# Quarter images for all groups: the second upsampling layer and the last layer of a preactivation chain of four convolutions

## The chip, the core and the metric

The kernel runs on one core of one Trainium2 chip. The metric is the device time of one execution in microseconds (us). A run's time is taken without a profiler; the profiled execution is a run of its own, with its own time.

## What is computed

The input is `x` of 16 samples, 32 channels, 128 x 128. Four layers follow each other, each with a normalisation before it and a residual around it: a recurrent layer along the diagonals (L0), an adder layer (L1: minus the sum of absolute differences between each 3 x 3 patch and each filter), a layer in the Hartley domain (L2: 32 x 32 modes are mixed), and a small encoder and decoder (L3). Only the end of L3 is touched by the change:

```python
def conv3x3(x, w, b):      # 3 x 3, padded, 32 -> 32 channels
def deconv2x2(x, w, b):    # 2 x 2 upsampling, 32 -> 32 channels
# five edge operators on x, normalised, 160 channels
y1 = maxpool2(conv1(edges))        # 64 x 64
y2, y3 = maxpool2(conv2(y1)), maxpool2(conv3(y2))   # 32 x 32, 16 x 16
y4 = conv4(y3)                     # 16 x 16
y5 = conv5(deconv1(y4))            # 32 x 32
y6 = conv6(deconv2(y5))            # 64 x 64
y7 = conv7(deconv3(y6))            # 128 x 128
# the output combines y7 with the normalised image
```

In the code a `deconv` and the `conv` behind it are one layer: `up5`, `up6` and `up7` compose their weights into 16 products of 32 x 32 channels (four output parities, four taps each) and small corrections at the image's edges.

## The kernel before

**Stages.** `stage0` does the recurrent layer (0 to about 690 us). `rest` does the others. In `Differences.run` each of the 16 images, in two halves, needs 72 tap arrays per half (2304 in all): relu(q - w) over 128 partitions and 8192 or 8320 elements, in float16. DVE makes some of them (`d_dve`, L760) and ACT the others (`d_act`, L757); PE sums each with 16 products (L647). DVE has three buffers for them, ACT two. Where PE would be idle between sums, products with zeros are put in (`keep_busy`, L677).

**Weaving.** The layers L2 and L3 work on groups of four samples (NG = 4). Their work is a generator, `After.work`, and the class `Weave` puts steps of it between the tap arrays. It keeps a planned time for PE, DVE and ACT. A step yields a positive number (PE time), a negative one (a wait) or `SUMMED` (wait until PE's sums are there), and adds its costs to `weave.dve` and `weave.act`; `later` and `on_act` put a step off. From the same plan comes the choice of the engine for each tap array. At the end `keep_order` fixes the order on every engine, so a wait at the head of an engine's queue holds all that stands behind it. Group g may start when image 4g + 3 is through; its parts in order are `forward` (loads `xh` at L1059 and products at L1110, mode mixing at L1221), `back` (L1295, L1345, residuals at L1320), `statistics` (L1491), `conv1` (L1874) with its pooled outputs, `small_layers` and `last`. Groups 0 to 2 are woven in; what is left of group 2 when the arrays end is played together with the whole of group 3 by `drain`, which takes the next step of whichever generator's planned time is lower. When group 2 is through, group 3 goes on alone (`weave.alone`).

**Layouts.** A tile with a plain layout has 4 samples x 32 channels on the partitions (`padded`). In a tile by quarters (`quartered`), the 128 partitions are 4 quarters of the image's rows x 32 channels, and the samples lie in the free dimension; `neighbours` copies each quarter's edge rows to the one next to it (L1812, L1814). Products are 32 x 32 blocks, 16 at a time: the row block of PE is a sample or a quarter, the column block is what becomes the output's partition block.

**up6.** Group 3 (`self.whole`) writes `y6` by quarters, through `to_quarters` and `evict` (L1789 on DVE, L1792 on ACT). Groups 0 to 2 write a plain `y6` through `upsampled` and `spread`: there the output's partition block is a parity (row, column), so that each bank of 512 sums is taken out in four pieces of 32 partitions, on DVE (L1778) or ACT (L1781). `up5` uses `spread` in all groups, with 256 elements a piece.

**The last layer.** Group 3 keeps its normalised image in SBUF, writes the output into it (`last_in_place`) and stores it by 8 rows of each quarter. Groups 0 to 2 read the normalised image back from DRAM by units of 32 rows (L1972, four transfers per unit, tiles `xr3`, two buffers): the partitions are four row blocks x 32 channels, the samples are in the free dimension. DVE combines (L2032), ACT adds the mean (L2002), and SP stores (L2011, sixteen transfers per unit). As the normalisation's numbers belong to a sample and channel, and the partitions do not have the samples here, a small product (L1984) with its operands (L1981, L1987) brings them into place first.

**SP's queue** carries nearly all transfers: the tiles `xq` and `q` of the adder layer, its stores, the group's loads and the output's stores, in one order. In the drain it carries the loads of group 3's image (L1282) ahead of group 2's `u_conv7` and `xr3`.

Of the kernel before, what the change touches and what calls it, by code (L numbers as in the profile page):

```python
# [7 lines left out]
F32 = mybir.dt.float32  # L8
F16 = mybir.dt.float16
I32 = mybir.dt.int32  # L10
AF = mybir.ActivationFunctionType
# [5 lines left out]
HW = H * W  # L17
# [945 lines left out]
class After:  # L963
# [16 lines left out]
    def work(self, groups):  # L980
        if 0 in groups:
            yield from self.prepare()
        for g in groups:
            with self.pool("g_sm") as sm:
                yield ("after", 4 * g + 3)
                if g not in self.scales:
                    yield -8.0
                self.stats3 = sm.tile([128, 2, 1], F32, name="stats3")
                self.shift3 = sm.tile([128, 1], F32, name="shift3")
                yield from self.forward(g)  # L990
                with ExitStack() as kept:
                    yield from self.encoder(g, kept)
                    if self.whole:
                        yield from self.last_in_place(g)
                    else:
                        yield from self.last(g, g + 1 if g + 1 in groups else None)

    def acc(self):

# [642 lines left out]
    def small_layers(self, cp, rp, y1, y2):  # L1642
# [3 lines left out]
        if not y1:  # L1646
            for n in ("conv3", "conv4"):
                wc[n] = replicated(nc, cp, self.a[n], 9, f"w_{n}")
            up5, up6 = self.up5.loaded(cp), self.up6.loaded(cp)
            y3 = self.quartered(cp, 16, "y3")  # L1650
            y4, y5 = (self.padded(cp, n, f"y{i}") for n, i in ((16, 4), (32, 5)))
            self.y6 = y6 = (self.quartered if self.whole else self.padded)(rp, 64, "y6")
            yield -7.0

        def conv(name, n, rows, pick, evict, taps=range(9), late=None):
# [93 lines left out]
            ),  # L1749
        )  # L1750
        yield from upsampled(y4, 16, up5, y5)
        yield from (to_quarters if self.whole else upsampled)(y5, 32, up6, y6)

    def padded(self, pool, n, name):
        nc, t = self.nc, pool.tile([128, n + 2, n + 2], F32, name=name)
# [15 lines left out]
    def spread(self, dst, src, blk, b, engine):  # L1771

        nc, weave = self.nc, self.weave
        for j in range(4):
            d, s = dst(slice(32 * blk, 32 * blk + 32), j), src[32 * j : 32 * j + 32]
            bj = b[32 * j : 32 * j + 32]
            if blk % 2 == 0 if weave.alone else engine is nc.vector:
                nc.vector.tensor_scalar(d, s, bj, None, ALU.add)  # L1778
                weave.dve += 0.3
            else:  # L1780
                nc.scalar.activation(d, s, AF.Identity, bias=bj)  # L1781
                weave.act += 0.45

    def evict(self, dst, src, b, blk, engine=None):

# [137 lines left out]
        for v in spreads:  # L1923
            weave.done(v)

    def last_in_place(self, g):

        nc, x = self.nc, self.image
        with self.pool("l_y") as yp:
            up = self.up7.loaded(yp)
            one = yp.tile([128, 1], F32, name="l_one")
            nc.vector.reciprocal(one, self.stats3[:, 1])
            nc.vector.tensor_scalar(one, one, up.bias, None, ALU.add)
            for unit in range(4):
                for pr in range(2):
                    acc = [self.acc() for _ in range(4)]
                    for pc in range(2):  # L1940
                        pick = lambda q: (2 * pr + pc, 16 * q + 4 * unit, 4, 256 * pc)
                        yield from up.round(self.y6, 64, acc, pick, 16)
                    yield SUMMED
                    for q in range(4):
                        first = 2 + 32 * q + 8 * unit + pr
                        v = x[:, first : first + 7 : 2, 2 : W + 2].rearrange("p r (w b) -> p r w b", b=2)
                        nc.vector.scalar_tensor_tensor(
                            v, acc[q].rearrange("p (b r w) -> p r w b", b=2, w=64), one, v, ALU.add, ALU.mult
                        )
                    yield -2.5  # L1950
                for q in range(4):
                    row = 32 * q + 8 * unit
                    v = x[:, 2 + row : 10 + row, 2 : W + 2]
                    nc.scalar.activation(v, v, AF.Identity, bias=self.stats3[:, 0])
                    to = self.out.offset + g * 4 * CHW + row * W
                    nc.sync.dma_start(bass.AP(self.out.tensor, to, [[HW, 128], [W, 8], [1, W]]), v)

    def last(self, g, following_group):

        nc, tc, cst, weave = self.nc, self.tc, self.cst, self.weave  # L1960
        with self.pool("l_y") as yp, self.pool("l_x", self.buffers["l_x"]) as xp:
            ahead = self.buffers["l_x"]
            y6 = self.y6
            up = self.up7.loaded(yp)

            def load(unit):
                xr = xp.tile([128, 4, 8 * PW], F32, name="xr3")
                t = self.d["xn"]
                for j in range(4):
                    first = t.offset + g * 128 * PADDED + (2 + 32 * unit + 8 * j) * PW  # L1970
                    rows = bass.AP(t.tensor, first, [[PADDED, 32], [32 * PADDED, 4], [1, 8 * PW]])
                    nc.sync.dma_start(xr[32 * j : 32 * j + 32], rows)  # L1972
                return xr

            def inner(x):
                return x.rearrange("p b (h w) -> p b h w", w=PW)[:, :, :, 2 : W + 2]

            xr = [load(unit) for unit in range(ahead)]

            rhs = yp.tile([128, 2, 4], F32, name="l_rhs")  # L1980
            nc.vector.tensor_tensor(rhs, bcast(self.stats3[:, :, 0], 2, 4), bcast(cst["m4_bc"], 1, 2), ALU.mult)  # L1981
            yield -2.0
            p = self.acc()
            nc.tensor.matmul(p[:, :8], cst["sel_c"], rhs.rearrange("p a b -> p (a b)"), start=True, stop=True)  # L1984
            yield SUMMED
            ms = yp.tile([128, 8], F32, name="l_ms")
            nc.vector.tensor_copy(ms, p[:, :8])  # L1987
            mean, istd = ms[:, 0:4], ms[:, 4:8]


            one = yp.tile([128, 4], F32, name="l_one")
            nc.vector.reciprocal(one, istd)
            nc.vector.tensor_scalar(one, one, up.bias, None, ALU.add)
            yield -4.0


            following = {}

            def done(x, unit):
                for blk in range(4):  # L2000
                    v = inner(x)[:, blk]
                    nc.scalar.activation(v, v, AF.Identity, bias=mean[:, blk : blk + 1])  # L2002
                weave.act += 4.4
                following[unit] = weave.later(4.0 if weave.alone else 14.0, lambda: store(x, unit))

            def store(x, unit):
                for blk in range(4):
                    for j in range(4):
                        first = self.out.offset + (g * 4 + blk) * CHW + (32 * unit + 8 * j) * W
                        rows = bass.AP(self.out.tensor, first, [[HW, 32], [W, 8], [1, W]])  # L2010
                        nc.sync.dma_start(rows, inner(x)[32 * j : 32 * j + 32, blk])  # L2011
                following[unit] = weave.later(10.0, lambda: reload(unit)) if unit + ahead < 4 else None

            def reload(unit):
                xr.append(load(unit + ahead))
                following[unit] = None

            def complete(unit):
# [2 lines left out]

            for unit in range(4):
                complete(unit - ahead)
                x = xr[unit]
                for pr in range(2):
                    acc = [self.acc() for _ in range(4)]
                    for pc in range(2):
                        yield from up.round(y6, 64, acc, lambda j: (2 * pr + pc, 16 * unit + 4 * j, 4, 256 * pc))
                    yield SUMMED
                    for blk in range(4):  # L2030
                        v = inner(x)[:, blk, pr::2].rearrange("p r (w b) -> p r w b", b=2)
                        nc.vector.scalar_tensor_tensor(  # L2032
                            v,
                            acc[blk].rearrange("p (b r w) -> p r w b", b=2, w=64),
                            one[:, blk : blk + 1],
                            v,
                            ALU.add,
                            ALU.mult,
                        )
                        weave.dve += 0.75  # L2040
                    yield -2.5
                following[unit] = weave.on_act(lambda x=x, unit=unit: done(x, unit))
# [168 lines left out]
```

## Time and profile before

| what | value |
|---|---|
| median of 3 runs | 6511.71 us (6506.15 to 6521.65) |
| the profiled execution's own time | 6506.94 us |
| its span, first to last instruction | 6505.2 us |
| busy: PE, DVE, ACT | 5343.1, 5475.0, 5312.8 us (82%, 84%, 82%) |
| tap arrays, on DVE and on ACT | 1673 and 631 |
| woven stage (arrays), about | 690 to 5651 us |
| group 2 and 3 together, group 3 alone | 5651 to 6042, 6042 to 6505 us |
| mean granted TensorE clock | 0.929 |

In the rows of the profile, a group of instructions has its line, engine and operation, then output <- input with partitions x elements, and the count after an x; behind the bar stand the busy time in us and the mean of one in ns, and behind the next bar the idle time of the engine just before such instructions, with what ended it. In a timeline the first number is the start and the second the length of a run of equal instructions, both in us. A matmul of 32-bit floats shows as two records, and so does its weight load. "issue" is a wait that no semaphore explains.

### The profile page before, as it was taken

To read this page: it belongs to the slowest core of one execution; us is meant where nothing else is said; L and a number is where in the kernel's file an instruction comes from. 1 tells how busy PE (TensorE), PEld (TensorE's weight loads), DVE (VectorE), ACT (ScalarE), POOL (GpSimd) and SP (SyncE) were. 2 spreads that over 40 slices of the span, in tenths; PEclk is the share of its full clock that TensorE was granted. 3 is DMA by queue.
4 is the path that set the end of the run, shared out by engine and by line. 5 is a ranking of instruction groups with operands and counts; after the bars stand their busy time and mean duration, and the time that the engine had idled before them with its cause. 6 is when DMAs were issued, how large, how long until landed. Compare 5 with 4: busy or idle time off the path is not lost.

```text
span 6505.2 us, 274662 instructions
## 1 busy us (share of the span) xinstructions
PE 5343.1 (82%) x129394; PEld 2805.1 (43%) x129394; DVE 5475.0 (84%) x6551; ACT 5312.8 (82%) x2816; POOL 65.6 (1%) x67
## 2 busy tenths in 40 slices
PE   3689677888877879998887889998878799977696
PEld 3576233344434433333344433334344443345594
DVE  7799899999999999999999889999989889744212
ACT  3899799999999989999999899999989899702001
POOL 0000000000000000000000000000000000000000
PEclk9999899999999889999989989999989899977898
DMA  7543323121154632222455522314545522344102
GB/s 314 218 173 126 91 51 82 46 57 45 32 140 124 197 120 87 66 74 68 110 166 165 176 79 70 97 42 92 146 128 172 171 58 62 101 139 121 35 4 65
DMA packets 366576, 700.87 MB, mean 108 GB/s; under 512 B 70852, under 2 KB 219332, under 8 KB 354564
## 3 DMA queue, kind: packets, MB, share of 16 engines
q1 hardware_dynamic: 357972, 648.87, 34.4%
q0 software_dynamic: 7040, 33.80, 1.6%
q8 instruction: 1012, 16.58, 1.1%
q14 instruction: 120, 0.98, 0.0%
q10 hardware_dynamic: 432, 0.64, 0.0%
HBM read 500.46 MB, written 182.69 MB: 105 GB/s over the span
## 4 chain that ended last, share of the span: by engine, by line
PE 41%; issue 25%; DVE 20%; ACT 8%; DMA 4%; SPq 1%; POOL 0%; DVEq 0%; ACTq 0%; POOLq 0%
PE acc L647 14%; PE acc L1874 13%; DVE d_dve L760 12%; ACT d_act L757 4%; PE acc L908 3%; PE pg L223 3%; ACT gt L237 2%; PE acc L1664 2%; ACT junk L198 1%; PE acc L1491 1%; PE acc L677 1%; DVE stat L124 1%; PE acc L662 1%; DMA v<-fold_d 1%; PE acc L1221 1%
## 5 line engine op out<-in xcount | busy, mean ns | idle before, releaser
L757 ACT ACTIVATE d_act<-q,neg 128x8192 f16<-128x8192 f16 (+1 forms) x631 | 4470.2, 7149 | 209.1 <-PE acc L647 190.1
L760 DVE TENSOR_SCALAR d_dve<-q,qw 128x8192 f16<-128x8192 f16 (+1 forms) x1673 | 3866.9, 2360 | 215.7 <-PE acc L647 195.1
L647 PE MATMUL acc<-d_dve,sel 128*32 128x512 f16 x26768 | 1862.5, 397 | 429.2 <-DVE d_dve L760 333.6
L647 PEld LDWEIGHTS <-sel 128*32 128x32 f16 x36864 | 984.7, 99 | 1968.1 <-issue 1291.7
L647 PE MATMUL acc<-d_act,sel 128*32 128x512 f16 x10096 | 713.7, 403 | 153.3 <-ACT d_act L757 142.4
L1874 PE MATMUL acc<-xp,wf 32*32 32x512 f32 x19200 | 721.1, 609 | 16.7 <-issue 15.8
L677 PE MATMUL acc<-q,zero 128*32 128x512 f16 x8584 | 582.7, 388 | 6.3 <-issue 6.3
L223 PE MATMUL pg<-h,wb 64*64 64x20 f32 (+15 forms) x8192 | 342.8, 306 | 61.0 <-DVE h L251 32.9
L237 ACT ACTIVATE gt<-pg,bias 128x20 f32<-128x20 f32 (+15 forms) x1024 | 332.6, 384 | 45.8 <-PE pg L223 43.5
L1874 PEld LDWEIGHTS acc<-xp,wf 32*32 32x32 f32 x19200 | 225.2, 103 | 315.9 <-issue 285.8
L908 PE MATMUL acc<-y,u_conv 32*32 32x256 f32 (+1 forms) x9984 | 313.0, 461 | 50.8 <-issue 33.8
L677 PEld LDWEIGHTS <-zero 128*32 128x32 f16 x8584 | 247.3, 99 | 229.3 <-issue 35.2
L1792 ACT ACTIVATE y<-pooled,b 128x128 f32<-128x128 f32 x112 | 39.7, 396 | 348.9 <-DVE pooled L1767 230.7
L223 PEld LDWEIGHTS pg<-h,wb 64*64 64x64 f32 x8192 | 252.8, 150 | 135.8 <-DVE h L251 79.5
L908 PEld LDWEIGHTS acc<-y,u_conv 32*32 32x32 f32 x9984 | 149.5, 111 | 151.3 <-issue 113.3
L223 PE MATMUL pg<-xn,wb 64*64 64x2 f32 (+63 forms) x4096 | 186.1, 292 | 27.9 <-issue 19.2
L1874 PE MATMUL acc<-image,wf 32*32 32x512 f32 x6400 | 207.3, 605 | 0.0
L1874 PEld LDWEIGHTS acc<-image,wf 32*32 32x32 f32 x6400 | 180.5, 103 | 24.1 <-issue 3.5
L1491 PE MATMUL acc<-xp 32*64 32x204 f32 (+2 forms) x6432 | 175.5, 341 | 13.5 <-issue 13.4
L1908 DVE TENSOR_TENSOR acc<-acc,cut 128x8 f32<-128x8 f32 x128 | 19.5, 166 | 194.0 <-PE acc L1874 194.0
L2002 ACT ACTIVATE xr<-xr,l_ms 128x1024 f32<-128x1024 f32 x48 | 51.5, 1145 | 152.3 <-DVE xr L2032 152.3
L1664 PE MATMUL acc<-y,w_conv 32*32 32x512 f32 (+2 forms) x4608 | 142.7, 476 | 26.5 <-issue 19.0
(248 smaller groups left out, 3891.8 us busy)
## 6 DMA issues: line engine op xcount, KB each, us to landing
q<-q_d SPq DMA_DIRECT2D x128, 536.2 KB, 9.7
xp<-xn_d SPq DMA_DIRECT2D x24, 2112.0 KB, 9.0
x_in<-in_x_dram SPq DMA_DIRECT2D x16, 2048.0 KB, 14.7
xn<-in_xs_dram SPq DMA_DIRECT2D x64, 512.0 KB, 7.2
res<-in_x_dram SPq DMA_DIRECT2D x64, 512.0 KB, 8.8
x_d<-res SPq DMA_DIRECT2D x64, 512.0 KB, 5.2
xq<-x_d SPq DMA_DIRECT2D x256, 128.0 KB, 4.4
xr<-x_d SPq DMA_DIRECT2D x256, 128.0 KB, 5.0
```

Of the source, the lines that this page charges most:

```text
L124: nc.vector.bn_stats(stat0[:, g, 8 * q + k, :], t[:, k * 512 : (k + 1) * 512])
L198: nc.scalar.activation(junk, flat(res, g)[:, 512 * half : 512 * half + 512], AF.Square, bias=away[:, g : g + 1], accum_out=squares[:, g, c ...
L223: nc.tensor.matmul(bank[c][q][64 * pair : 64 * pair + 64, :, :width], wb[half, 4 * kind + KIND[q]].rearrange("p b o -> p (b o)"), v[half], ...
L237: nc.scalar.activation(gt[:, q, :, :n], bank[c][q][:, :, :n], AF.Tanh if q == G else AF.Sigmoid, bias=bias[:, KIND[q] : KIND[q] + 1],)
L647: self.nc.tensor.matmul(acc[k][32 * j : 32 * j + 32, :], self.sel16[:, i // 9, :], d[:, row : row + 4, c : c + W], start=first, stop=last,)
L677: self.nc.tensor.matmul(acc[k][32 * j : 32 * j + 32, :], self.zero, q[:, :4, :W], start=False, stop=False)
L757: nc.scalar.activation(dst, src, AF.Relu, bias=self.neg[:, i : i + 1])
L760: nc.vector.tensor_scalar(dst, src, self.qw[:, i : i + 1], 0.0, ALU.subtract, ALU.max)
L908: nc.tensor.matmul(acc[blk][32 * j : 32 * j + 32, o : o + rows * n], t[part, 4 * par + tap, :], own[:, top : top + rows, left : left + n], ...
L1491: nc.tensor.matmul(gram[blk][j : j + width, at : at + n], xp[part, l, 2 + j : 2 + j + width], xp[part, rows, j : j + width + 4], start=sta ...
L1664: nc.tensor.matmul(acc[blk][32 * j : 32 * j + 32, : rows * n], wc[name][part, tap, :], pick(part, blk, j)[:, tap // 3 : tap // 3 + rows, t ...
L1874: nc.tensor.matmul(acc[blk][32 * j : 32 * j + 32, :], tap_of("all", tap)[rows], xp[rows, at + apart * j + kh : at + apart * j + kh + 4, kw ...
```

## The change

All groups now write `y6` by quarters: `to_quarters` with `evict` for everyone. `last_in_place` and `last` become one function. For groups 0 to 2 the last layer's partitions are now the samples and channels, a unit is 8 rows of each quarter, a load takes one transfer per unit (the same bytes) and a store four; the mean and the deviation are used as they are. In group 3 the addition of the mean and the stores are put off by `on_act`. `spread` tells the planner other costs.

```diff
@@ After.work
-                    if self.whole:
-                        yield from self.last_in_place(g)
-                    else:
-                        yield from self.last(g, g + 1 if g + 1 in groups else None)
+                    yield from self.last(g, g + 1 if g + 1 in groups else None)
@@ small_layers
-            self.y6 = y6 = (self.quartered if self.whole else self.padded)(rp, 64, "y6")
+            self.y6 = y6 = self.quartered(rp, 64, "y6")
...
-        yield from (to_quarters if self.whole else upsampled)(y5, 32, up6, y6)
+        yield from to_quarters(y5, 32, up6, y6)
@@ spread
-                weave.dve += 0.3
+                weave.dve += s.free_size() / 960 + 0.2
...
-                weave.act += 0.45
+                weave.act += s.free_size() / 960 + 0.25
@@ last
-    def last_in_place(self, g):
...
+    def last(self, g, following_group):
+        nc, weave = self.nc, self.weave
+        mean = self.stats3[:, 0]
+        with self.pool("l_y") as yp, ExitStack() as ring:
+            up, ahead = self.up7.loaded(yp), self.buffers["l_x"]
+            xr, following = [], {}
+            if not self.whole:
+                xp = ring.enter_context(self.pool("l_x", ahead))
+
+            def load(unit):
+                xr.append(xp.tile([128, 4, 8 * PW], F32, name="xr3"))
+                t = self.d["xn"]
+                first = t.offset + g * 128 * PADDED + (2 + 8 * unit) * PW
+                nc.sync.dma_start(xr[unit], bass.AP(t.tensor, first, [[PADDED, 128], [32 * PW, 4], [1, 8 * PW]]))
+
+            def rows(unit):
+                if self.whole:
+                    x = self.image[:, 2 : H + 2, :].rearrange("p (q r) w -> p q r w", q=4)
+                    return x[:, :, 8 * unit : 8 * unit + 8, 2 : W + 2]
+                return xr[unit].rearrange("p q (r w) -> p q r w", w=PW)[:, :, :, 2 : W + 2]
+
+            if not self.whole:
+                for unit in range(ahead):
+                    load(unit)
             one = yp.tile([128, 1], F32, name="l_one")
             nc.vector.reciprocal(one, self.stats3[:, 1])
             nc.vector.tensor_scalar(one, one, up.bias, None, ALU.add)
+            yield -4.0
+
+            def done(x, unit):
+                for q in range(4):
+                    nc.scalar.activation(x[:, q], x[:, q], AF.Identity, bias=mean)
+                    if self.whole:
+                        store(x, unit, q)
+                weave.act += 4.4
+                after = weave.later(4.0 if weave.alone else 14.0, lambda: stored(x, unit)) if not self.whole else None
+                following[unit] = after
+
+            def store(x, unit, q):
+                to = self.out.offset + g * 4 * CHW + (32 * q + 8 * unit) * W
+                nc.sync.dma_start(bass.AP(self.out.tensor, to, [[HW, 128], [W, 8], [1, W]]), x[:, q])
...
             for unit in range(4):
+                complete(unit - ahead)
+                x = rows(unit)
                 for pr in range(2):
                     acc = [self.acc() for _ in range(4)]
                     for pc in range(2):
                         pick = lambda q: (2 * pr + pc, 16 * q + 4 * unit, 4, 256 * pc)
                         yield from up.round(self.y6, 64, acc, pick, 16)
                     yield SUMMED
                     for q in range(4):
+                        v = x[:, q, pr::2].rearrange("p r (w b) -> p r w b", b=2)
                         nc.vector.scalar_tensor_tensor(
                             v, acc[q].rearrange("p (b r w) -> p r w b", b=2, w=64), one, v, ALU.add, ALU.mult
                         )
                         weave.dve += 0.75
                     yield -2.5
+                following[unit] = weave.on_act(lambda x=x, unit=unit: done(x, unit))
...
```

More of the change, by code (lines that the diff above doesn't have):

```diff
@@ L1924, in conv1 @@
             weave.done(v)
-    def last_in_place(self, g):
-        nc, x = self.nc, self.image
-        with self.pool("l_y") as yp:
-            up = self.up7.loaded(yp)
+    def last(self, g, following_group):
[19 more added lines that the diff above has]
+                    load(unit)
             one = yp.tile([128, 1], F32, name="l_one")
@@ L1936, in last_in_place, with stored, reload, complete @@
             nc.vector.tensor_scalar(one, one, up.bias, None, ALU.add)
+            yield -4.0
[10 more added lines that the diff above has]
+                nc.sync.dma_start(bass.AP(self.out.tensor, to, [[HW, 128], [W, 8], [1, W]]), x[:, q])
+            def stored(x, unit):
+                for q in range(4):
+                    store(x, unit, q)
+                following[unit] = weave.later(10.0, lambda: reload(unit)) if unit + ahead < 4 else None
+            def reload(unit):
+                load(unit + ahead)
+                following[unit] = None
+            def complete(unit):
+                while following.get(unit):
+                    weave.done(following[unit])
             for unit in range(4):
+                complete(unit - ahead)
+                x = rows(unit)
                 for pr in range(2):
@@ L1944, in last_in_place @@
                     for q in range(4):
-                        first = 2 + 32 * q + 8 * unit + pr
-                        v = x[:, first : first + 7 : 2, 2 : W + 2].rearrange("p r (w b) -> p r w b", b=2)
+                        v = x[:, q, pr::2].rearrange("p r (w b) -> p r w b", b=2)
                         nc.vector.scalar_tensor_tensor(
                             v, acc[q].rearrange("p (b r w) -> p r w b", b=2, w=64), one, v, ALU.add, ALU.mult
-                        )
-                    yield -2.5
@@ L1951, in last_in_place @@
[L1951 to L2018, printed above, removed]
-                while following.get(unit):
-                    weave.done(following[unit])
[L2022 to L2038, printed above, removed]
```

## The prediction

> **What bounds the kernel now.** I read the busy table by stretches first, then the groups of instructions by shape, then the timeline around the first up6 layer and around the image load. In the table the columns after the window are its length, then the busy time of PE, PEld, DVE, ACT and POOL, the granted clock, the DMA share and the GB/s.
>
> ```profile
> 690.00:1850.00 1160.00, 934.39 (x16746) 451.87 (x16749) 1144.94 (x886) 1138.80 (x178) 0.00 (x0) 0.96 0.23 58
> 1850.00:2996.00 1146.00, 1012.32 (x23716) 455.09 (x23709) 1063.95 (x899) 1085.54 (x243) 18.04 (x15) 0.94 0.38 109
> 2996.00:3045.00 49.00, 37.06 (x776) 14.54 (x776) 47.00 (x45) 42.17 (x22) 0.00 (x0) 0.88 0.13 31
> 3250.00:3300.00 50.00, 39.54 (x474) 16.83 (x473) 42.38 (x38) 38.30 (x7) 0.00 (x0) 0.86 0.93 236
> 4700.00:5651.00 951.00, 826.29 (x19618) 385.49 (x19623) 864.85 (x719) 879.69 (x201) 18.16 (x17) 0.94 0.38 110
> 5651.00:6042.00 391.00, 286.46 (x9172) 180.05 (x9172) 153.66 (x402) 57.60 (x92) 5.21 (x10) 0.76 0.52 140
> ```
>
> From 690 to 5651 us the tap arrays of the adder layer are made on DVE and ACT; both are busy 90% to 99% in every stretch, so **the woven stage is bound by DVE and ACT together**, and what groups 0 and 1 do on them costs span. From 5651 us on, the drain, DVE is busy 154 of 391 us and ACT 58: there work on them is nearly free, and PE with its waits decides. Groups 0 and 1 run up6 and the last layer in the woven stage (L1778 from 2999 and from 4420 us), group 2 in the drain (5811 to 6042 us).
>
> ```profile
> L1778 DVE TENSOR_SCALAR y<-acc,b_conv 32x512 f32<-32x512 f32 x48 | 36.0, 750 | 7.4 <-PE acc L908 6.6
> L1781 ACT ACTIVATE y<-acc,b_conv 32x512 f32<-32x512 f32 x48 | 35.5, 740 | 131.5 <-PE acc L908 130.9
> L1789 DVE TENSOR_SCALAR y<-acc,b_conv x4: 743/748/754, 6395.8 to 6406.9; 128x512 f32<-128x512 f32 x4
> L1792 ACT ACTIVATE y<-acc,b_conv x4: 681/690/697, 6395.8 to 6406.8; 128x512 f32<-128x512 f32 x4
> L1812 DVE COPY y<-y x27: 186/284/289, 2904.6 to 6408.4; 32x256 f32<-32x256 f32 x15, 32x64 f32<-32x64 f32 x12
> ```
>
> These rows hold most of the price. Group 3 already writes y6 by quarters (last three), groups 0 to 2 do not (first two): an eviction on 32 partitions takes as long as one on 128.
>
> **What the Trainium skill says.** "ScalarE: Activation LUTs", section "What ACT_TABLE_LOAD costs", prices an activation with a bias operand by elements per partition: 280 ns + 0.833 ns each, 707 ns for 512. The trace agrees: 740 ns on 32 partitions, 690 on 128. "VectorE: DVE Perf Modes", section "Mode 2×_2P — use both read ports for one tensor", says PSUM has one read port for DVE, so one element a cycle; 750 and 748 ns for 512 agree. "Runtime: NRT & Kernel Launch", section "Instruction fetch mechanics", says engines' instructions are refilled by DMA in 16 KiB blocks of 256 instructions. The page's instruction queue, 1012 packets for 16.58 MB, is that size, and the drain's timeline below shows PE going forward 128 matmul records, with their loads one block, at a time.
>
> **The change part by part.** *The up6 layer, per group.* DVE loses 16 x 750 ns = 12.0 us and gains 4 x 748 = 3.0, six copies between quarters of 284 ns (1.7), and for the edges 2 x 278 + 2 x 118 instead of 4 x 113 ns (0.3). The last layer loses two small DVE operations (L1981, L1987: 0.16 + 0.17). Net 7.3 us less. ACT loses 16 x 740 = 11.8 and gains 4 x 690 = 2.8: 9.1 us less. For groups 0 and 1: DVE 14.6, ACT 18.2.
>
> *The plan.* The order is written by the planner, whose costs also change (0.3 us for a spread becomes 0.47 for 256 elements, where the trace has 485 ns). The order of the changed kernel has the tap arrays shared out anew: DVE makes one array more in all (15 short ones more at 2349 ns, 14 long ones fewer at 2380: +1.9 us), ACT one fewer (15 short fewer at 7119, 14 long more at 7224: -5.7). Sum: DVE -12.7 us, ACT -23.9 us. An array takes 2.36 us on DVE and 7.15 on ACT, so a microsecond of DVE is worth 0.75 of span and one of ACT 0.25: 0.75 x 12.7 + 0.25 x 23.9 = **15.5 us**. If DVE alone sets the pace it is 12.7, if ACT alone 23.9.
>
> *Stalls around up6.* The plan counted 16 x 0.3 = 4.8 us for what takes DVE 12.0 there and 8 for up5, so DVE fell behind the fixed order and ACT waited:
>
> ```profile
> 3016.90 6.11 ACT L1781 ACTIVATE y<-acc,b_conv 32x512 f32<-32x512 f32 x8 [5.88 <-PE acc L908]
> 3037.88 5.95 ACT L1781 ACTIVATE y<-acc,b_conv 32x512 f32<-32x512 f32 x8 [0.70 <-PE acc L908]
> ```
>
> With plan and trace now within 0.5 us on these rows, these 6.6 us (ACT) and 1.4 (DVE), and 1.1 and 0.5 in group 1, may go: at the same weights at most 3.3 us. I take 2. What is late next is the wait of the first product of up6 for the evictions of up5, which stay 16 DVE operations.
>
> *Stores and loads.* Per group 64 stores of 128 KB become 16 of 512 KB and 16 loads become 4; bytes stay. All sit on SP, in front of other transfers:
>
> ```profile
> 3242.01 9.56 SPq L2011 DMA_DIRECT2D out_dram<-xr  x16
> 3251.68 1.92 SPq L342 DMA_DIRECT2D q<-q_d  x4
> 3253.83 26.30 SPq L1059 DMA_DIRECT2D xh<-x_d  x6
> ```
>
> Sixteen issues take 9.56 us; four of the 512 KB form take 4 x 0.38 (L1956) = 1.5. Behind them stand the next q tile and the next group's xh. PE stands at L1110 for xh, the arrays' sums stand behind it on PE, and in 3250 to 3300 us ACT is idle 11.7 us in one piece and DVE 4.5. The loads can leave 8 us earlier, but they are 1 MB each and take over 4 us apiece, so only the first come earlier. At 0.75 and 0.25 all of it is 6.3 us; 4660 to 4700 us shows little of it (ACT 5.2 idle). I take **3**, between 0 and 6. The other stores have arrays running beside them and no waiter: 0, and if that cover were gone, 8 us of SP per bunch. A larger load is waited for as a whole, as the four together were (10.7 us to landing, the 2112 KB window loads 9.0): 0.
>
> *PE in the woven stage.* Up6 goes from 128 to 256 products of half the width (0.058 and 0.029 us of PE time per record, so 14.9 us a group either way) and 64 to 96 edge products. The order drops 188 filler products (L677), worth 582.7/8584 x 188 = 12.8 us of PE, which were there only to fill waits: cost 0; if fillers were really PE's slack, up to +3 us a group. One 8-column product per group (L1984) and its wait go: 0, other work stood beside it.
>
> *The drain.* When the arrays end, 448 conv1 products of group 2 are left instead of 464: no head start. Its evictions shorten by 12 of 32 operations on two engines, but PE was elsewhere:
>
> ```profile
> 5838.92 1.46 PE L1295 MATMUL acc<-cw,zi 32*32 32x32 f32 x128 [3.42 <-issue]
> 5863.32 1.54 PE L1295 MATMUL acc<-cw,zi 32*32 32x32 f32 x128 [7.84 <-issue]
> 5872.55 1.54 PE L1295 MATMUL acc<-cw,zi 32*32 32x32 f32 x128 [7.69 <-issue]
> ```
>
> With the DMA engines full (share 0.99 in 5820 to 5880, the image and xr loads), PE gets a block each 6.7 us on average. Up6 of group 2 is now (256 + 96) - (128 + 64) = 160 products longer, 640 instructions or 2.5 blocks; half lie in this stretch: 1.25 x 6.7 = 8 us if the loads are still running, 4 at the 3.5 us a block takes after. Against it stand some 4 us of shorter waits for banks (round 2 took 8.27 us for 83 records, behind L1778's 6.1). Net 0, between -10 and +12. Group 3 alone (6042 to 6505) does the same work in the same order: 0.
>
> *Sum:* -15.5 - 2 - 3 + 0 = -20.5. The profiled execution took 6506.9 us (span 6505.2 and 1.7 around it): 6486.4. The median shown, 6511.7, is 4.8 above it, so I forecast **6491 us** for the median. A measurement here can tell about 0.2%, 13 us, from no change.
>
> **The rivals.** *The freed time becomes idle time* (no change). The order is fixed, and behind up6 all of it is planned anew. DVE is idle 1.3% in 690 to 1850 us, where no group runs, but 82 of 1146 us in 1850 to 2996 and 86 of 951 in 4700 to 5651, where plan and chip disagree. A new plan draws these anew; a tenth of both later ones is 17 us either way. For it: the size of those idles. Against: the work removed is where both engines are full. It gives about 6510 (6499 to 6525).
>
> *PE starves in the drain* (slower). In the new order the second half of up6 and the first two rounds of up7 (176 products, 704 instructions, 2.75 blocks) all stand ahead of group 3's first L1345 products; before, only one round of up6 did. If the loads last until PE has come through, that is 8 us + 2.75 x 9.4 (the spacing of the last two blocks) = 34 us on group 3's chain. Against the lowest woven gain, 12.7, it ends 21 us slower, 6533. It decides from some 26 us more of full DMA engines on; before they emptied near 5876, two us before PE was through L1295. Bytes do not grow, which speaks against it.
>
> *Twice the gain.* ACT's saving counts in full because DVE was the late one, the idles at up6 and xh go whole, the drain gains 8: 23.9 + 6.3 + 8 = 38, giving 6474.
>
> **How the numbers follow.** Forecast 0.52, twice the gain 0.13, idle 0.24, starving 0.11. The forecast's own ends (-12.7 + 5 and -24 - 3 - 6) give 6479 to 6504, a tenth of it within 0.2%; a little of the idle case falls over. Faster 0.63, same 0.24, slower 0.13. The range 6468 to 6520 leaves out the starving case and the tails.
>
> **What would show it.** Right: DVE's busy time falls by about 20 us in all (36.0 for 9.0 in evictions, copies +5.1), ACT's by about 33; the last array's sums end some 18 to 24 us before 5649; ACT's wait at up6 is under 2 us; four stores take under 3 us of SP. Wrong: the woven stage ends within 8 us of 5651 although the busy times fell (then idle took it), or the drain is over 866 us instead of 854.

## The result, and the profile after

The changed kernel took 6473.1 us (median of 6 runs, 6465.7 to 6476.6), the kernel before 6508.9 us (6 runs, 6493.4 to 6521.6) on the same chip. The ratio is 0.994, 95% interval 0.993 to 0.9951: **faster by 36 us by the medians, 39 by the ratio, 0.6%**. The forecast was 6491 us, a gain of 20.5; the sign was right and the time lies in the range, but the gain by the medians is 1.75 times the forecast's. The profiled execution took 6473.5 us, with a span of 6471.7.

The busy line of the page after (before, in the table above: 5343.1, 5475.0, 5312.8):

```profile
PE 5326.5 (82%) x130160; PEld 2805.8 (43%) x130160; DVE 5455.2 (84%) x6528; ACT 5276.5 (82%) x2779; POOL 58.7 (1%) x67
```

The busy table by stretches after, with the columns of the prediction's table. The woven stage now ends at 5624 us (before, the last tap array ended at 5646), and the stretches in the middle are those around up6 of group 0 and around the load of group 1's image:

```profile
690.00:1850.00 1160.00, 936.82 (x16782) 452.68 (x16774) 1146.88 (x890) 1140.41 (x178) 0.00 (x0) 0.96 0.23 58
...
2996.00:3040.00 44.00, 41.49 (x1202) 21.56 (x1203) 42.55 (x30) 39.22 (x10) 0.00 (x0) 0.96 0.29 111
3240.00:3290.00 50.00, 41.75 (x600) 20.75 (x600) 47.90 (x57) 50.00 (x8) 0.00 (x0) 0.97 0.52 117
4680.00:5624.00 944.00, 821.79 (x19512) 371.00 (x19511) 869.63 (x708) 879.35 (x200) 17.41 (x15) 0.94 0.38 111
5624.00:6018.00 394.00, 301.69 (x9902) 196.91 (x9899) 148.33 (x397) 48.95 (x80) 5.79 (x11) 0.78 0.46 140
```

In the stretch around the image load ACT is busy 50.00 of 50 us, where before it was busy 38.30. The evictions, by line and shape (count, then the shortest, median and longest in ns, and the first and last start in us):

```profile
L1786 DVE TENSOR_SCALAR y<-acc,b_conv x16: 740/746/754, 3009.0 to 6374.9; 128x512 f32<-128x512 f32 x16
L1789 ACT ACTIVATE y<-acc,b_conv x16: 673/686/700, 3009.0 to 6374.9; 128x512 f32<-128x512 f32 x16
L1775 DVE TENSOR_SCALAR y<-acc,b_conv x56: 473/482/520, 2988.2 to 6354.4; 32x256 f32<-32x256 f32 x56
```

All four groups' evictions are now the long ones on 128 partitions, 16 on each engine where there were 48 + 4, at the price expected. In the timeline of group 0's up6, ACT takes two at a time and waits once, 2.02 us, where it waited 5.88 and 0.70 before:

```profile
3009.00 1.25 ACT L1789 ACTIVATE y<-acc,b_conv 128x512 f32<-128x512 f32 x2
3010.15 14.12 ACT L757 ACTIVATE d_act<-q,neg 128x8192 f16<-128x8192 f16 x2
3026.30 1.28 ACT L1789 ACTIVATE y<-acc,b_conv 128x512 f32<-128x512 f32 x2 [2.02 <-PE acc L908]
```

SP's queue at the end of group 0's last layer, with four stores where there were sixteen (9.56 us before):

```profile
3203.25 3.96 SPq L1967 DMA_DIRECT2D out_dram<-xr  x4
3212.67 10.83 SPq L1056 DMA_DIRECT2D xh<-x_d  x4
```

So far this reads like the forecast's own mechanism. What it doesn't tell is where the other 16 us come from.

### The profile page after: what moved, and what is told of

Read it like the earlier page. It is cut to its first block, busy times and chain, and to the rows that moved or that the text cites. A ratio compares the mean times of both kernels' runs of the same rounds, so it can differ in the third digit from the quotient of the medians.

```text
span 6471.7 us, 275922 instructions
## 1 busy us (share of the span) xinstructions
PE 5326.5 (82%) x130160; PEld 2805.8 (43%) x130160; DVE 5455.2 (84%) x6528; ACT 5276.5 (82%) x2779; POOL 58.7 (1%) x67
## 4 chain that ended last, share of the span: by engine, by line
PE 26%; issue 11%; DVE 8%; ACT 3%; DMA 2%; SPq 0%; POOL 0%; DVEq 0%; ACTq 0%; POOLq 0%
PE acc L1871 10%; PE acc L647 9%; DVE d_dve L760 4%; PE acc L908 3%; ACT d_act L757 2%; PE acc L1661 1%; PE acc L1488 1%; PE acc L1292 1%; DMA xm_d<-xm 0%; PE acc L1218 0%; PE acc L662 0%; DVE pooled L1764 0%; PE acc L934 0%; DMA v<-fold_d 0%; PE acc L1844 0%
## 5 line engine op out<-in xcount | busy, mean ns | idle before, releaser
L760 DVE TENSOR_SCALAR d_dve<-q,qw 128x8192 f16<-128x8192 f16 (+1 forms) x1674 | 3868.3, 2360 | 215.3 <-PE acc L647 193.1
L908 PE MATMUL acc<-y,u_conv 32*32 32x256 f32 x10752 | 318.4, 435 | 60.7 <-issue 45.1
L662 PE MATMUL acc<-q,sel 32*32 32x512 f16 x4608 | 158.4, 393 | 4.0 <-issue 4.0
```

The costliest lines, as they stand in the source:

```text
L662: self.nc.tensor.matmul(acc[k][32 * j : 32 * j + 32, :], self.sel16[rows, 8, :], q[rows, row : row + 4, kw : kw + W], start=False, stop=False,
L760: nc.vector.tensor_scalar(dst, src, self.qw[:, i : i + 1], 0.0, ALU.subtract, ALU.max)
L908: nc.tensor.matmul(acc[blk][32 * j : 32 * j + 32, o : o + rows * n], t[part, 4 * par + tap, :], own[:, top : top + rows, left : left + n], ...
```

## The experiments

The theory at the start was the forecast's: the gain is DVE and ACT work taken out of the woven stage, and little of it lies in the drain. Rivals were: the drain; the new order itself; the stores' issues on SP; and the loads, which the prediction had costed at nothing. The ratio is to the kernel before, run beside each on the same chip; "us" is the ratio's distance from 1 times 6509. e1 to e4 ran on one chip (median of before 6495 us), c1 and e5 to e7 on a second (6506), e8 to e11 on a third (6507), so that a comparison across these three rests on the ratios.

| kernel | ratio, 95% interval | us |
|---|---|---|
| the change | 0.994 [0.993, 0.9951] | -39 |
| the change again, c1 | 0.9941 [0.9927, 0.9955] | -38 |
| e1, group 2 alone changed | 0.9985 [0.9979, 0.9992] | -10 |
| e2, all but group 2 changed | 0.995 [0.9938, 0.9963] | -33 |
| e3, up6's evictions in pieces again | 0.997 [0.9958, 0.9981] | -20 |
| e4, loads and stores split again | 0.9988 [0.9981, 0.9994] | -8 |
| e5, loads split again | 1.001 [1.0003, 1.0016] | +7 |
| e6, stores split again | 0.9926 [0.9913, 0.9938] | -48 |
| e7, pieces, loads and stores all again | 1.0005 [0.9996, 1.0015] | +3 |
| e8, loads split by quarter | 0.9934 [0.9921, 0.9946] | -43 |
| e9, kernel before, new planner costs | 1.0072 [1.0057, 1.0086] | +47 |
| e10, up5 shared | 0.9947 [0.9932, 0.9963] | -34 |
| e11, up5 shared, stores split | 0.9928 [0.9911, 0.9945] | -47 |

A second table locates the differences. From the trace's records of the tap arrays I took the time between the ends of the 1101st, 1297th, 1681st, 1873rd and last array; the first and third of these stretches hold group 0's and group 1's up6 and last layer, and the drain runs from the last array to the end. Up to the last array, c1 and e2 to e8 have the changed kernel's order of instructions on PE, DVE and ACT (in e3 and e7 with the pieces in the place of an eviction), and e1 that of the kernel before, so within either family the rows compare piece by piece. In the drain c1, e6 and e8 keep that order too; e2, e3, e4, e5 and e7 take steps there in another one. Each is one profiled execution; the change and c1, equal kernels, differ by up to 4 us in a stretch, 10 in the second. The executions of e1, c1 and e3 are the fastest of their kernels' runs, 14, 8 and 9 us below the median, that of e9 is the slowest, 8 above.

| kernel | group 0's last | between | group 1's last | to the last array | drain |
|---|---|---|---|---|---|
| before | 442.8 | 863.0 | 421.9 | 964.4 | 859.2 |
| e1, group 2 alone changed | 447.6 | 856.1 | 422.7 | 961.1 | 838.7 |
| the change | 422.9 | 882.5 | 424.0 | 952.0 | 847.7 |
| c1, the same again | 423.5 | 872.7 | 421.6 | 948.1 | 849.0 |
| e2, all but group 2 changed | 424.5 | 880.2 | 420.9 | 944.2 | 847.6 |
| e3, evictions in pieces | 432.7 | 870.6 | 431.0 | 943.4 | 837.2 |
| e4, loads and stores split | 436.2 | 870.1 | 431.4 | 946.9 | 853.9 |
| e5, loads split | 440.3 | 868.4 | 437.2 | 947.5 | 866.7 |
| e6, stores split | 427.5 | 874.8 | 420.3 | 946.5 | 843.9 |
| e7, pieces and both split | 441.4 | 873.0 | 445.2 | 949.8 | 852.4 |
| e8, loads split by quarter | 421.8 | 872.3 | 418.4 | 947.0 | 851.6 |
| e9, before, new costs | 453.3 | 879.7 | 430.7 | 970.8 | 873.7 |

**Which groups: e1 and e2.** In e1 groups 0 and 1 keep the plain `y6` and the old last layer, and the planner's costs of `spread` are the old ones throughout; in e2 only group 2 keeps the old layers, with the new costs:

```diff
+                self.plain = g < 2          # e2: g == 2
-                    yield from self.last(g, ...)
+                    last = self.last_plain if self.plain else self.last
+                    yield from last(g, ...)
-            self.y6 = y6 = self.quartered(rp, 64, "y6")
+            self.y6 = y6 = (self.padded if self.plain else self.quartered)(rp, 64, "y6")
-        yield from to_quarters(y5, 32, up6, y6)
+        yield from (upsampled if self.plain else to_quarters)(y5, 32, up6, y6)
```

> Groups 0 and 1 as before, group 2 (which runs up6 and the last layer in the drain) as changed; on every engine the order up to the last tap array is that of the kernel before, instruction for instruction. If the drain holds a third of the gain, as the two profiles suggest (drain 859 us before, 847 after), it is 10 to 14 us faster than before. If the drain difference is only where the woven stage happened to leave the transfers, within 5 us of before. If the drain holds most of the gain: 25 us or more faster.

> Groups 0, 1 and 3 as changed, group 2 as before; the order up to the last tap array is that of the changed kernel, instruction for instruction. It holds the woven part of the gain alone. Forecast's theory (evictions, stalls and stores in the woven stage): 18 to 24 us faster than before. If the drain holds it: under 8 us faster. With the first run the two parts should add up to the whole, about 36 us.

Measured: -10 us and -33 us, together about the whole. The woven groups are worth some 30, against the 20.5 of the forecast, and group 2 in the drain 5 to 10, which the prediction had at 0 with a bound of -10. The drain's own time does not tell this clearly: with group 2 in the old layout e2's lasted 847.6 us, as short as the changed kernel's 847.7 and 849.0, where before it took 859.2. So how the woven stage leaves the drain to start counts too, or chance in single executions.

**The evictions: e3.** The changed kernel, with up6's sums of groups 0 to 2 taken out in four pieces of 32 partitions as before, and the plan told nothing of it, so that the order stays.

```diff
+                    planned = weave.dve, weave.act
+                    for j in range(4):
+                        part = slice(32 * j, 32 * j + 32)
+                        self.evict(d[part], v[part], up.bias[part], blk, engine)
+                    weave.dve = planned[0] + (weave.dve - planned[0]) / 4    # and act
```

> As changed, but in groups 0 to 2 each eviction of up6 is four of 32 partitions (32 instructions a group again), and the planner is told the cost of one, so the order stands as it is. This puts back 9 us of DVE and 8.3 of ACT per group, and the gap between plan and chip. Theory of the evictions: for groups 0 and 1 it costs 2 x 9 = 18 us where DVE falls behind a fixed order, at least 13; in the drain another 0 to 6, so 13 to 24 us slower than the changed kernel. If the gain came from the new order or from the stores, under 6 us slower.

The groups of e3 by shape, against 16 of 128 x 512 on each engine after (the busy time in us is followed by the mean in ns):

```profile
L1791 DVE TENSOR_SCALAR y<-acc,b_conv 32x512 f32<-32x512 f32 x48 | 35.9, 748 | 19.6 <-PE acc L908 18.7
L1794 ACT ACTIVATE y<-acc,b_conv 32x512 f32<-32x512 f32 x48 | 33.0, 687 | 144.6 <-PE acc L908 143.9
```

Measured: about 20 us slower than the change, by the ratios. Against c1 the second table shows 9 us more in each of the two stretches with a woven up6 and none elsewhere, in the drain least of all. So, with everything else as in the changed kernel, the evictions are worth what the prediction gave them with the stalls at up6 (15.5 + 2), and the surplus is something else.

**The transfers: e4, then e5 and e6 apart.** The same bytes, and up to the last array the same order on PE, DVE and ACT; only the loads go out in four transfers of 32 partitions (e5), or the stores of groups 0 to 2 (e6), or both (e4).

```diff
-                nc.sync.dma_start(xr[unit], bass.AP(t.tensor, first, [[PADDED, 128], [32 * PW, 4], [1, 8 * PW]]))
+                for j in range(4):                                   # e4, e5, e7
+                    part = bass.AP(t.tensor, first + 32 * j * PADDED, [[PADDED, 32], [32 * PW, 4], [1, 8 * PW]])
+                    nc.sync.dma_start(xr[unit][32 * j : 32 * j + 32], part)
...
+                for j in range(4):                                   # e4, e6, e7, e11
+                    part = bass.AP(self.out.tensor, to + 32 * j * HW, [[HW, 32], [W, 8], [1, W]])
+                    nc.sync.dma_start(part, x[32 * j : 32 * j + 32, q])
```

> As changed, but in groups 0 to 2 each load is four transfers of 32 partitions again and each unit's stores sixteen; the order on the other engines stays. Forecast's theory: 3 us (0 to 6) slower than the changed kernel, from the loads of the next group's rows behind 16 issues of about 0.6 us. If the long queue on SP was the cost: over 10 us slower.

> The changed kernel as it is, timed on the same chip as the three kernels sent with it, so that they can be set against it. About 0.994 of before (36 to 39 us faster) if the first comparison holds on another chip.

> As changed, but in groups 0 to 2 each load of the normalised image is four transfers of 32 partitions (16 a group instead of 4, the same bytes); stores and all else as changed. The kernel with both split ran at 0.9988 of before, so shape and number of transfers are worth far more than the 3 us of the forecast. Theory of the slow load: in the trace a 4224-byte packet takes 313 ns where the transfer spans 32 partitions and 185 where it spans 128, and PE waits for its instructions meanwhile; then this kernel is 12 to 20 us slower than the changed one. Theory of SP's queue (the time to issue 16 stores): under 4 us slower.

> As changed, but in groups 0 to 2 the stores of a unit are sixteen transfers of 32 partitions; loads as changed. Theory of SP's queue: 15 to 25 us slower than the changed kernel. Theory of the slow load: 3 to 10 us slower (512-byte packets took 34 ns on 32 partitions and 29 on 128).

e4 gave 31 us of the 39 back, where the forecast's theory allowed 6. e5 and e6, run beside c1, say which half it was: with split loads the whole gain is gone (50 us by the medians, 6513.3 against 6463.4), with split stores nothing is lost (6457.3). In the second table e5 loses 17 us in group 0's last layer, 16 in group 1's and 18 in the drain, and nothing in between.

Why a load matters so is in the DMA view, for 30 us around the first two units' loads of group 0 (two of 2112 KB, or eight of 528 KB). A queue's line gives packets, MB, and the share of the 16 DMA engines' time that the packets took; a line of issues gives count, size and the median us to landing. First c1, then e5, then before:

```profile
q1 hardware_dynamic: 1275, 4.98, 44.4%
...
xr<-xn_d SPq DMA_DIRECT2D x2, 2112.0 KB, 11.6
```
```profile
q1 hardware_dynamic: 1296, 4.74, 74.4%
...
xr<-xn_d SPq DMA_DIRECT2D x8, 528.0 KB, 13.0
```
```profile
q1 hardware_dynamic: 1296, 4.74, 76.1%
...
xr<-xn_d SPq DMA_DIRECT2D x8, 528.0 KB, 13.6
```

The bytes are about equal, but e5 and before hold the engines for three quarters of the window, c1 for less than half. By the trace's packet records the 1024 packets of 4224 bytes take 166 ns each in c1, 321 in e5, 333 in before. In the same view the rate while they run is 382 to 439 GB/s in c1 and mostly 180 to 265 in the others. The landing times of single transfers hardly show it, 11.6 us against 13.0 and 13.6, as those of the four transfers overlap; from the first issue to the last landing on record the two units take 14.5 us in c1, 22.1 in e5 and 23.0 in before.

What is late for it is not the layer that waits for the load. These are the waits in group 0's last layer, summed (us, times, longest), first of c1, then of e5:

```profile
PE acc L647 <- ACT d_act L757: 13.9, 10, 2.7
...
PE acc L908 <- issue: 3.1, 2, 2.4
...
PE acc L647 <- issue: 1.5, 4, 0.5
...
ACT d_act L757 <- PE acc L647: 3.1, 1, 3.1
```
```profile
PE acc L908 <- issue: 10.5, 6, 3.8
PE acc L647 <- issue: 8.7, 4, 4.8
...
PE acc L647 <- ACT d_act L757: 2.7, 2, 1.5
...
ACT d_act L757 <- PE acc L647: 15.6, 6, 5.5
```

In these rows PE's waits without a semaphore grow from 4.6 to 19.2 us, and ACT then waits for PE's sums 12.5 us longer; DVE's waits for them (L760 and L628) grow from 7.0 to 17.8. PE's own waits for ACT's arrays shrink from 13.9 to 2.7: PE is now the late one. It is so in the other kernels too: over the whole first stretch of the second table PE's waits without a semaphore sum to 12.6 to 21.0 us in the eight kernels with loads over 128 partitions and to 24.5 to 32.8 in the six with loads over 32.

What these waits are for can be read from the packets. PE's instructions come by the same 16 DMA engines, in packets of 16,384 bytes on a queue of their own. Of PE's waits without a semaphore that are longer than 0.5 us, from 690 us on, 153 of 160 in c1 and 159 of 166 in e5 end 1.0 to 1.8 us after such a packet has landed, 1.4 in the median; of moments taken evenly over the same time only 13% lie so. So these waits are for PE's instructions. That the split loads are what makes them late is shown by e5 in the total and not wait by wait: only 7 to 9 of e5's 20 us of such waits in this layer overlap a load's flight, and no run took the blocks out of the way.

One more thing goes along. In the first stretch of the second table the granted clock was 0.936 in c1 and 0.915 in e5, and PE was busy for 358.1 and 364.6 us with the same work. No run held the clock fixed, so whether the waits lower it, or part of the loss comes from the clock itself, is open.

**Evictions and transfers together: e7.** The edits of e3 and of e4 at once: evictions in pieces, of which the plan is told nothing, and loads and stores split.

> As changed, but with up6's evictions in four pieces (the planner not told) and with loads and stores split in groups 0 to 2: the work on DVE, ACT and SP of before in the order of the changed kernel. If evictions (17 to 19 us by the third run) and transfers (some 30 us by the fourth) add up, it is 45 to 50 us slower than the changed kernel and 8 to 12 slower than before: the new order by itself would then cost about 10. If they overlap in the same waits, it stands at before, 36 to 39 us slower than the changed one.

Measured: 1.0005, the kernel before. The two costs don't add up: by the ratios e3 lost 19 us and e5 45, e7 only 42. Against c1 in the second table they overlap in group 0's layers (9 and 17, together 18), add up in group 1's (9 and 16, together 24), and in the drain the pieces cost nothing. The changed order, with the old layout's costs put back, is worth nothing by itself.

Read the other way, the evictions are worth 19 us only where the loads are whole (one transfer over 128 partitions). Beside split loads they are worth less: e4 and e7, which differ in the pieces alone, are 11 us apart on two chips, and e5, on e7's chip with the shorter evictions but whole stores, is even 4 behind e7. And a cost put back in the new order doesn't say where the new kernel is faster than the old one: e7's five stretches add up to 3562 us and those of before to 3551, but group 1's last layer takes 445.2 in e7 and 421.9 in before, as short as in the change. Against before, the change and c1 gain 19 to 20 us in group 0's layers, nothing in group 1's, and 12 to 16 in the stretch to the last array, where no layer was changed; they lose 10 to 20 in "between".

**Partitions or number of transfers: e8.** Again four transfers a unit with the same packets as in e5, but each over all 128 partitions.

```diff
+                for q in range(4):
+                    nc.sync.dma_start(xr[unit][:, q], bass.AP(t.tensor, first + 32 * q * PW, [[PADDED, 128], [1, 8 * PW]]))
```

> The changed kernel, and only its loads of the normalised image go out as four transfers per unit again, but now each of them covers all 128 partitions and one quarter's 8 rows (528 KB each, the same 512 packets of 4224 bytes per unit, the same number of transfers as e5). The order on PE, DVE, ACT and POOL is the changed kernel's. Theory A (what costs is that a transfer covers 32 partitions): packets keep some 175 ns instead of 320, and the time stays at the changed kernel's ratio, 0.992 to 0.996 of before. Theory B (what costs is the number of transfers, the SP time of 12 more issues per group and their overhead): as e5, ratio about 1.001, 45 us slower than the changed kernel, with packets of 320 ns or the same wait at the products.

Its DMA view over 30 us (eight transfers; the window holds more other packets, 5.71 MB in all):

```profile
q1 hardware_dynamic: 1644, 5.71, 53.5%
...
xr<-xn_d SPq DMA_DIRECT2D x8, 528.0 KB, 7.7
```

Measured: 0.9934, no loss; the same 1024 packets took 167 ns. So **it is the 32 partitions, not the number of transfers**. The Trainium skill states this, on the page "SBUF — State Buffer", section "Door 1: The DMA port swizzle (why `[64,N]` ≈ `[32,N]`)": a transfer reaches as many of SBUF's 16 DMA ports as its partitions touch, 8 for 32 partitions, and it gives 189 GB/s for partitions 0 to 31 against 328 for 128 at 1 MiB, with limits of 218 and 436. The page's "Can I just issue two DMAs to hit both halves?" adds that transfers side by side don't make up for it. Both agree with the trace: half the rate, also with four such transfers queued at once.

**The plan alone: e9.** The kernel before with the new costs of `spread`, replanned.

```diff
-                weave.dve += 0.3
+                weave.dve += s.free_size() / 960 + 0.2
-                weave.act += 0.45
+                weave.act += s.free_size() / 960 + 0.25
```

> The kernel before, in which only the planner's costs of a spread piece are those of the change (0.47 and 0.52 us for 256 elements, 0.73 and 0.78 for 512 instead of 0.3 and 0.45); what is computed, moved and stored is as before, the order of the tap arrays is planned anew. Theory A (the gain is the shorter evictions and the faster loads): the ratio is 1.000 within 0.003; only the 1.4 and 6.6 us of waits at group 0's up6 and less in group 1's can go, at most 3.3 us. Theory B (a good part of the gain is the new shares and the truer plan): at least 10 us faster, 0.998 or lower. The redrawn idle stretches can move it by some 10 us to either side in both.

Measured: 47 us slower, in every stretch of the second table, though both engines' busy times are those of before within 1 us (DVE 5475.5, ACT 5313.7). From 3300 to 4100 us ACT's waits for PE's sums, first of before, then of e9:

```profile
ACT d_act L757 <- PE acc L647: 39.1, 17, 11.1
```
```profile
ACT d_act L757 <- PE acc L647: 63.9, 20, 23.5
```

Neither theory had this. Costs nearer the trace's gave a worse order; the prediction's rival of redrawn idle stretches is real and, at 47 us, larger than the 17 it was priced at. Why this draw is bad was not settled. Nor did a run draw the changed kernel's order with the old costs of `spread`, or otherwise anew, so how much of its gain depends on its own draw isn't known beyond what e7 says of it.

**Towards a better version: e10 and e11.** up5's pieces taken out by DVE and ACT in turn (24 operations move, eight in each of groups 0 to 2), and the same with split stores.

```diff
-                        nc.vector if n == 16 or blk % 2 else nc.scalar,
+                        nc.vector if blk % 2 else nc.scalar,
```

> The changed kernel, in which up5's pieces go to DVE and ACT in turn (before: all to DVE); 24 operations of 32 x 256 leave DVE for ACT in all, planned anew. By the engines' weights, 12 operations in the woven groups take 12 x 0.485 = 5.8 us off DVE and lay about 12 x 0.53 = 6.4 on ACT: 0.75 x 5.8 - 0.25 x 6.4 = 2.8 us faster than the changed kernel, and the first product of up6 waits about 3 us less in each woven group. Ratio 0.993 if the changed kernel stands at 0.994. Rival: the new plan redraws the idle stretches and up5 was not waited for; then it lies within 10 us of the changed kernel to either side.

> As e10, and the stores of groups 0 to 2 in four pieces of 32 partitions as in e6; order on PE, DVE and ACT as e10. If e6's lead over the changed kernel (6 to 10 us) comes from the split stores, it is found again here: 6 to 10 us faster than e10, ratio about 0.991 to 0.992. If it was chance between runs, e11 equals e10 within 4 us; if a store's issue time on SP counts, e11 is some 3 to 6 us slower.

e10 stands at 0.9947, beside the change; the 3 us expected can't be told. e11 is 12 us ahead of e10, as e6 is 6 to 10 ahead of c1, and e4 (loads and stores split) is 14 ahead of e5 by the ratios, on another chip: three times the same sign, but the intervals of e6 and c1, and of e11 and e10, overlap. The lowest ratios found are thus those of e6 and e11, 0.9926 and 0.9928; that they are better than the change is not shown. Why sixteen stores should be better than four is open: in group 0's last layer (3088 to 3240 us) the 512-byte packets took 33 ns each in e6 and 28 in c1, and sixteen issues held SP 9.14 us, four 3.96.

## Why the prediction was right, and where its size was off

**Evictions, -15.5, and stalls at up6, -2: right in size, but not on their own.** Beside whole loads e3 puts both at some 20 us. DVE's busy time fell by 19.8 us and ACT's by 36.3 (expected about 20 and 33), the last array ended 22 us earlier (18 to 24), and ACT's wait at up6 was 2.02 us, just over the 2 of its sign. But e5 has the same short evictions beside loads over 32 partitions, and this is its busy line:

```profile
PE 5350.0 (82%) x130160; PEld 2809.8 (43%) x130160; DVE 5456.4 (84%) x6528; ACT 5278.7 (81%) x2779; POOL 58.9 (1%) x67
```

DVE and ACT have 18.6 and 34.1 us less to do than before, and yet the last array ends at 5646.1 us, where it ended at 5645.9. That is the prediction's own sign of being wrong, "the woven stage ends within 8 us of 5651 although the busy times fell (then idle took it)". With the loads as they were, the rest of the change lost 7 us (e5) or, with the stores as they were too, gained 8 (e4), and not 20.5. So part of the hit was luck: the term priced at nothing is what let the others through.

**Loads, 0: this is the mis-sized term.** The step reads "A larger load is waited for as a whole, as the four together were": it asked who waits for the load, and took the landing times of single transfers, which are nearly equal (10.7 and 9.0 us), for those of the four together. It didn't ask what else travels on the DMA engines while the load runs. Halving the time of a packet is worth about 16 us in each of the three groups in this order, 45 to 50 us in all (e5 against c1). With the stores split along with the loads it is 31 (e4 against the change), and beside evictions in pieces 23 (e7 against e3). The prediction had the elements: it priced PE's blocks at 6.7 us with full DMA engines and 3.5 without, but applied that only to the drain, and held the transfers' time for fixed because the bytes were. The port count of the skill's page was not used for it.

**Stores on SP, -3: refuted, with its mark.** Four stores took 3.96 us of SP, not under 3, and splitting them again cost nothing (e6). The wait that the step wanted to remove is indeed gone: around the load of group 1's image ACT's idle time fell from 11.7 us (in the 65 us from 3250 of before) to 0.0 (62 us from 3223 after). But in e6, with sixteen stores at 9.14 us, it is 1.1, and in e4 3.1, while e1, which has the order of before up to there, still has 12.2. What removed it is the new order; that it was given back in "between" (863 before, 873 to 882 after) is possible and not shown.

**Drain, 0 (-10 to +12): within its bounds, at the lower end.** e1 gives -10, and e2 lacks 5 to 6 us of the whole. In the first 295 us of the drain PE's waits without a semaphore at group 3's products back from the modes, first of before, then of c1, then of e5:

```profile
PE acc L1295 <- issue: 32.2, 7, 7.8
```
```profile
PE acc L1292 <- issue: 25.6, 8, 4.4
```
```profile
PE acc L1292 <- issue: 32.2, 8, 6.9
```

They shrink with the whole loads and are back with split ones, and e5's drain is 18 us longer than c1's, though not all in the same order of steps. That points to group 2's loads here too, though e2, with the old loads, has as short a drain; what the 2.5 extra blocks of up6 cost was not measured apart.

**The rivals.** "Freed time becomes idle" is what e5 shows, for another reason than a new draw: PE was late. A new draw alone can cost 47 us (e9). "PE starves in the drain" was wrong in sign, for the reason it named itself as its condition: the DMA engines are busy for a shorter time, not a longer one (a share of 0.46 of the first 394 us of the drain, 0.52 of 391 before). "Twice the gain" hit the size, 38 us, for another reason: it had no term for the loads.

**Two readings beside the sum** were off. DVE and ACT are not busy 90% to 99% in every stretch of the prediction's table: in the two short ones ACT was busy 86% and 77% of the time, and DVE 85% in the second. And of group 2's 32 evictions of up6, 24 go away, 12 on each engine, where "12 of 32 operations on two engines" can be read as 12 in all.

## What to carry to other kernels

Price a transfer twice: by who waits for it, and by how long it holds the DMA engines that others ride on, PE's instructions among them. A tile filled in pieces of 32 partitions held them for twice as long here as the same tile filled over 128 partitions at once, whatever the number of transfers; the landing times of single transfers hid it, the queue's share of the engines' time beside its bytes showed it. Where an order is planned ahead, separate an operation's cost from the luck of a new plan by keeping the order fixed while the cost is put back. And put costs back together as well as one by one: the long evictions cost 19 us alone and 11 at most beside split loads, which one cost at a time would not have told.

## What was unexpected of the hardware

A load over 32 partitions ran at half the rate of one over 128 (packets of 4224 bytes 321 to 333 ns against 166), but the 512-byte packets of the stretch with the stores much less (33 against 28 ns). And PE waited for its own instructions in the middle of the woven stage, where it awaited no data: 14.6 us more such waits in one group's last layer with split loads than with whole ones, and from 690 us on some 295 to 331 us in all, of which 274 to 310 ended 1.0 to 1.8 us after an instruction packet had landed (c1 and e5).
